# Earlier first steps for the partial sums of a graph layer: 2, 5, 8, 11 tiles in place of 3, 6, 9, 12

## The chip, the cores and the metric

The kernel runs on one core of a Trainium2 chip. The metric is the device time of one execution in microseconds (us). Before the change it is 1529.51 us, the median of three runs (1527.91 to 1533.11).

## What is computed

There are 6250 nodes with 64 features and 206,250 edges, sorted by the node `dst` that they belong to (padded to 206,336 edges, 1612 tiles of 128). For every edge a first layer takes the features of its `dst` node and its own 64 attributes; the hidden rows are then added up by the node `src`, which is in no order; a second layer, a residual and a layer norm follow per node.

```python
msg = jnp.concatenate([src_node_features[col], edge_attr], axis=1)   # col = dst
h = jax.nn.relu(msg @ W1a.T + b1a)
h = h @ W1b.T + b1b
sums = jax.ops.segment_sum(h, row, num_segments=n_nodes)             # row = src
agg = sums / jnp.maximum(counts, 1.0)[:, None]
z = jax.nn.relu(jnp.concatenate([src_node_features, agg], axis=1) @ W2a.T + b2a)
out = jnp.concatenate([z @ W2b.T + b2b, src_node_features], axis=1) @ Wr.T + br
x = _layernorm(x + out)
```

The kernel uses that `W1b` is linear and applies it after the sum, so that what is scattered and summed are rows of 128 hidden values, a 1 for the count and the node's number within its bin (130 floats). Nodes lie in 49 bins of 128.

## The kernel before, in words

**Blocks.** The edges are worked through in 124 blocks of 13 tiles. In a block TensorE (PE) computes the first layer (`hidden`, L1461, one matmul a tile, which the trace shows as two records). ScalarE (ACT) applies the relu into one of `ROWS` = 4 buffers `orow`, used in turn, and puts the node's number beside it (`low_bits`, L1452). VectorE (DVE) and PE work out a slot in DRAM for each row (`bins_of`, `counts_of`, `slots`). GpSimd (POOL) writes each tile of 128 rows into its slots with one indirect DMA (`scatter`, L1513). In blocks 2 to 109, six or nine of the 13 tiles are first joined into groups of four rows of one bin ("fours", `join`, L1348 and L1363, scattered by L1485); the others are "direct rows". So a block has 13 scatters (blocks 0, 1 and 110 to 123), 9 (six tiles joined) or 7 (nine tiles joined: blocks 9, 11, ... 25 and 34, 42, 50, ... 98). The scatters of block k - `LEAD` (2) are written into the program in block k. A row buffer is free for block k once the scatter of block k - 4 has landed.

**Partial sums.** Each bin's rows fill its slots in order, so early tiles of a bin are full long before the last block. `Step` objects say which tiles can be summed from which block on: for each number in `FULL[0]`, a step of direct rows ends at that many tiles of a bin and is ready at the first block by which every bin has at least as many (`low_of`); `FULLQ` does the same for fours. A stage of the two opens `LATE` (3) blocks after the later of them. `groups_of` cuts a stage into groups of at most 3 bins and 12 tiles (`SUMS`, `TILES`). A group is read back from DRAM by SyncE (SP, `read`, L1593, into 9 buffers `rt`), its nodes' numbers are turned into a matrix of ones by DVE (`nodes_of`, L1627), PE multiplies and adds (`summed`, L1647, two records a tile), and `collect` adds the result to `part`.

**What sets the order.** PE, ACT, DVE and SP keep the order in which the program is written. A small planner spreads the groups over the blocks: per block it hands out no more tiles than `RATES` allows (18 in a block with six joined tiles, 10 with nine, 55 with none), and no more than are left divided by the blocks to the next opening:

```python
until = min(o for o in opens if o > k)
credit += min(RATES[joined(k)], max(tiles_in(queue) - credit, 0) / (until - k))
while queue and credit > 0:
    groups_at[k].append(queue.pop(0))
    credit -= tiles_in(groups_at[k][-1:])
credit = min(credit, 0)
```

What the planner gives to block k is read at the end of block k and summed in block k + 1. After block 123 come the groups that are left (`NGR`, 124), then the 17 last groups, three tiles a piece, each followed by the second layer of its bins (`Nodes`).

**src.** The numbers in `src` are loaded into the memory of the `rt` buffers at first; `bins` (L761, L762) splits them into a bin and a place in the bin, in five parts at the blocks of `bins_at`. All of it must be done before `rt` is used for the first read.

Of the kernel before, what the change touches and what calls it, by code (L numbers as in the profile page):

```python
# [453 lines left out]
NEAR = 8  # L454
HEAD = 117
NEXT = 468
FULL = ((3, 6, 9, 12), (1,), ())
BIG = 2.0**20
LATE = 3
RD = 6  # L460
# [14 lines left out]
PACED = range(PRE, 123)  # L475
SIDES, ENATS, CHUNK = 2, 2, 2
ON_ACT = 1
FULLQ = (3, 6, 9, 11, 13)
NODES = 8
FIRST = 4  # L480

# [8 lines left out]
def fast_path(  # L490
# [39 lines left out]
    NT = srcT.shape[1]  # L530
# [35 lines left out]
    def by_bin(of_bin, of_rest):  # L566
        return [of_bin] * (NB - 1) + [of_rest]
# [9 lines left out]
    def low_of(b, n, first=0):  # L577
        _, mean, dev = edges_of(b, n, first)
        return max(0, int(mean - dev)) // P
# [9 lines left out]
    def quads_low(b, n):  # L589
        _, mean, dev = quads_of(b, n)  # L590
        return max(0, int(mean - dev)) * QUAD // P
# [10 lines left out]
    for e, n in enumerate(EPOCHS):  # L602
# [15 lines left out]
        ep_.steps, lo = [], by_bin(0, 0)  # L618
        for t in FULL[e]:
            at = next(k for k in range(n) if low_of(0, k, ep_.first) >= t)  # L620
# [24 lines left out]
    qep.steps, lo = [], by_bin(0, 0)  # L645
    for t in FULLQ:
        at = next(k for k in range(qep.end + 1) if quads_low(0, k) >= t)
# [129 lines left out]
    with (  # L777
# [253 lines left out]

        NBAD = 15 + 5 * NE + 2 * sum(map(len, FULL)) + 2 * len(FULLQ)
        bad = const.tile([P, NBAD], F32, name="bad")
# [797 lines left out]
        nodes_at = {AHEAD_FROM + EVERY * i: b0 for i, b0 in enumerate(range(0, NB, CHUNK))}  # L1831
        assert JOIN_FROM - 3 < AHEAD_FROM - 1 and max(nodes_at) < JOIN_TO

        bins_at = {NEAR - 2: (HEAD, NEXT), 22: (NEXT, 754), 24: (754, 1040), 26: (1040, 1326), 28: (1326, NT)}
        range_at = {4: (0, ALU.min), 5: (1, ALU.max)}
        assert NEXT % (SEG * BLK) == 0 and NEXT // BLK > max(bins_at) + 3
        for g in range(3):
# [392 lines left out]
```

## Time and profile before

| what | us |
|---|---|
| median of three runs | 1529.51 |
| lowest, highest | 1527.91, 1533.11 |
| the profiled execution, its time | 1534.22 |
| its span from the first to the last instruction | 1532.4 |
| PE busy | 1440.7 (94%) |
| DVE busy | 1341.7 (88%) |
| POOL busy | 1128.8 (74%) |
| ACT busy | 1114.6 (73%) |

The profile is that of one execution. Busy shares are means over the span. Time in which an engine issues a DMA does not count as busy, which matters for POOL here. A row of the timeline joins neighbours of one kind: start, duration, engine, line, operation, and how many records; in brackets stands how long the engine was idle before, and what ended that.

### The profile page before, as it was taken

The page shows a single profiled execution, that of the slowest core. Times are in us where ns is not written, and L with a number is a line of the kernel's source. Part 1 is how long each engine was busy: PE and PEld are TensorE (multiplying, and loading weights), DVE is VectorE, ACT ScalarE, POOL GpSimd, SP SyncE. Part 2 cuts the span into 40 slices and gives each one's busy share as a digit, 9 for nine tenths or more (in the row PEclk, how much of TensorE's full clock was granted, in tenths as well). Part 3 has the DMA queues.
Part 4 walks back from the last instruction along what each step waited for, and adds up shares of the span by engine and source line. Part 5 has one row for each costly group of instructions (what it writes and reads, how often), then busy time and mean ns, then how long its engine had stood idle before and what let it go on. Part 6 is the DMA issues. An engine that isn't in the chain of part 4 may idle for free.

```text
span 1532.4 us, 33764 instructions
## 1 busy us (share of the span) xinstructions
PE 1440.7 (94%) x11008; PEld 1274.8 (83%) x11008; DVE 1341.7 (88%) x2882; ACT 1114.6 (73%) x2413; POOL 1128.8 (74%) x1198
## 2 busy tenths in 40 slices
PE   5989999987999999999989998999999999999997
PEld 4767777766888988888878888989888899999896
DVE  8789999887898988979889898999999988788787
ACT  3689999996898888878878887887887744332004
POOL 6777777777777777777777777777777777777734
PEclk9899999998999999999999999999999999999999
DMA  8798998967788888777877767777677899999884
GB/s 206 221 301 284 302 303 288 308 188 257 238 262 256 251 253 270 221 229 224 231 238 214 233 213 244 237 227 250 210 242 229 279 322 320 345 343 310 264 275 115
DMA packets 255427, 390.92 MB, mean 255 GB/s; under 512 B 43412, under 2 KB 186838, under 8 KB 255242
## 3 DMA queue, kind: packets, MB, share of 16 engines
q1 hardware_dynamic: 206874, 265.50, 58.7%
q0 software_dynamic: 47840, 122.94, 22.8%
q8 instruction: 90, 1.47, 0.4%
q14 instruction: 95, 0.78, 0.2%
q10 hardware_dynamic: 528, 0.22, 0.1%
HBM read 213.72 MB, written 174.78 MB: 254 GB/s over the span
## 4 chain that ended last, share of the span: by engine, by line
PE 57%; DMA 16%; ACT 11%; DVE 7%; issue 5%; POOL 2%; SPq 1%; DVEq 0%; ACTq 0%; POOLq 0%
PE place L1647 22%; PE place L1348 11%; DMA rows<-orow,rowidx 9%; PE place L1461 9%; PE place L1363 8%; DMA rt<-rows 3%; DMA rows<-orow,qidx 3%; ACT orow L1366 2%; ACT marks L1314 2%; ACT marks L1318 1%; DVE marks L1302 1%; POOL rows L1513 1%; DVE oh L1627 1%; ACT orow L1465 1%; ACT rhs L1414 1%
## 5 line engine op out<-in xcount | busy, mean ns | idle before, releaser
L1513 POOL DMA_INDIRECT rows<-orow,rowidx x910 | 878.3, 965 | 288.0 <-issue 142.5
L1647 PE MATMUL place<-rt,oh 128*128 128x129 f32 x3952 | 483.7, 277 | 15.3 <-ACT orow L1366 5.9
L1647 PEld LDWEIGHTS place<-rt,oh 128*128 128x128 f32 x3952 | 467.7, 193 | 27.2 <-DVE oh L1627 8.3
L1627 DVE TENSOR_TENSOR oh<-ramp,rt 128x768 f32<-128x768 bf16 (+4 forms) x391 | 309.6, 824 | 42.4 <-DMA rt<-rows 41.3
L1465 ACT ACTIVATE orow<-place 128x512 f32<-128x512 f32 (+2 forms) x263 | 142.5, 542 | 224.5 <-PE place L1461 219.3
L1485 POOL DMA_INDIRECT rows<-orow,qidx x234 | 226.1, 966 | 71.3 <-issue 19.8
L1302 DVE TENSOR_TENSOR marks<-quad_ramp,ramp 128x1024 fp32r<-128x1024 f32 x234 | 273.4, 1213 | 1.5 <-ACT z_act L1310 1.5
L1363 PE MATMUL place<-mv,rj 128*128 128x130 f32 x1872 | 242.7, 280 | 33.9 <-ACT orow L1465 20.6
L1348 PE MATMUL place<-marks,side 128*128 128x512 f32 x702 | 267.5, 410 | 0.0
L1461 PE MATMUL place<-mv,rhs 124*128 124x128 f32 x1820 | 262.5, 289 | 4.7 <-ACT orow L1465 3.8
L1363 PEld LDWEIGHTS place<-mv,rj 128*128 128x128 f32 x1872 | 223.1, 192 | 44.5 <-ACT orow L1465 24.5
L1348 PE MATMUL place<-marks,rest 128*64 128x512 f32 x702 | 240.2, 396 | 0.0
L1461 PEld LDWEIGHTS place<-mv,rhs 124*128 124x128 f32 x1820 | 229.6, 197 | 6.2 <-ACT orow L1465 4.0
L1348 PEld LDWEIGHTS place<-marks,side 128*128 128x128 f32 x702 | 134.3, 191 | 51.6 <-issue 2.0
L1366 ACT ACTIVATE orow<-place 128x260 f32<-128x260 f32 x468 | 163.7, 389 | 13.4 <-PE place L1363 4.1
L1314 ACT ACTIVATE marks<-quad_ramp,z_act 128x512 fp32r<-128x512 f32 x234 | 168.9, 722 | 6.1 <-PE place L1348 2.7
L1318 ACT ACTIVATE marks<-marks,ones 128x512 fp32r<-128x512 f32 x234 | 169.8, 725 | 4.1
L1121 DVE TENSOR_TENSOR_SCAN had<-ramp,bins 128x400 bf16<-128x400 bf16 (+2 forms) x124 | 127.2, 1026 | 13.7 <-ACT orow L1452 1.7
L1353 ACT COPY rj<-place 128x512 f32<-128x512 f32 x234 | 133.3, 570 | 1.9 <-PE place L1348 1.9
L1348 PEld LDWEIGHTS place<-marks,rest 128*64 128x64 f32 x702 | 96.0, 137 | 38.6 <-issue 0.8
L1414 ACT ACTIVATE rhs<-rhs,ones 60x896 f32<-60x896 f32 (+2 forms) x116 | 123.7, 1066 | 3.7
L1412 ACT ACTIVATE rhs<-rhs,from_win 60x896 f32<-60x896 bf16 (+2 forms) x116 | 123.6, 1065 | 2.9
(197 smaller groups left out, 1594.7 us busy)
## 6 DMA issues: line engine op xcount, KB each, us to landing
rt<-rows SPq DMA_DIRECT2D x194, 390.0 KB
rt<-rows SPq DMA_DIRECT2D x97, 325.0 KB
rows<-padrow SPq DMA_DIRECT2D x24, 1040.0 KB
rhs<-in_edgeT SPq DMA_DIRECT2D x90, 224.0 KB
enat<-in_edgeJ SPq DMA_DIRECT2D x90, 192.0 KB
rows<-orow,rowidx POOLq DMA_INDIRECT x910
rt<-rows SPq DMA_DIRECT2D x40, 260.0 KB
rt<-rows SPq DMA_DIRECT2D x48, 195.0 KB
```

The lines of the kernel that those rows point to most:

```text
L1302: nc.vector.tensor_tensor(m[:, :n, :], all_q[:, None, :].to_broadcast([P, n, QUAD * P]), z[:, :n, None].to_broadcast([P, n, QUAD * P]), op ...
L1314: nc.scalar.activation(m[:, t, :], all_q, AF.Square, bias=z_acts[k][:, i * JOIN + t : i * JOIN + t + 1], scale=-1.0)
L1318: nc.scalar.activation(m[:, t, :], m[:, t, :], AF.Relu, bias=ones[:, :1], scale=-1.0)
L1348: done[k, f"turn{i}"] = nc.tensor.matmul(ps[: w.shape[1], :], w, m[:, t, :], start=t + p == 0, stop=last and p == 1).ins.name
L1363: done[k, f"join{i}"] = nc.tensor.matmul(ps[:, j, :], rj[:, (g0 + j) * P : (g0 + j + 1) * P], m, start=True, stop=True).ins.name
L1366: nc.scalar.activation(mrow[:, g0 : g0 + 2, :], ps, AF.Relu)
L1461: done[k, c] = nc.tensor.matmul(ps[:, j, :], rhs[:WIDE, of * P : (of + 1) * P], m[:WIDE, :H], start=True, stop=True).ins.name
L1465: nc.scalar.activation(orow_of(k, k0, n)[:, :, :H], ps[:, :n, :], AF.Relu)
L1485: s = nc.gpsimd.indirect_dma_start(out=qep.rows.rearrange("(q r) f -> q (r f)", r=QUAD), out_offset=bass.IndirectOffsetOnAxis(ap=qidx[:, q ...
L1513: s = nc.gpsimd.indirect_dma_start(out=ep_.rows, out_offset=bass.IndirectOffsetOnAxis(ap=rowidx[:, k % RING * BLK + j : k % RING * BLK + j ...
L1627: nc.vector.tensor_tensor(res[:, at_tile : at_tile + nb * n, :], ramp[:, None, :].to_broadcast([P, nb * n, P]), node[:, :, None].to_broadc ...
L1647: m = nc.tensor.matmul(of_bin(b), oh[:, at, :], rows, start=i == 0, stop=i == len(of) - 1)
```

## The change

The change gives new values to two tables of ends, and moves the last four parts of `src` four blocks ahead, to 18, 20, 22 and 24 from 22, 24, 26 and 28.

```diff
-FULL = ((3, 6, 9, 12), (1,), ())
+FULL = ((2, 5, 8, 11), (1,), ())
...
-FULLQ = (3, 6, 9, 11, 13)
+FULLQ = (2, 5, 8, 11, 13)
...
-        bins_at = {NEAR - 2: (HEAD, NEXT), 22: (NEXT, 754), 24: (754, 1040), 26: (1040, 1326), 28: (1326, NT)}
+        bins_at = {NEAR - 2: (HEAD, NEXT), 18: (NEXT, 754), 20: (754, 1040), 22: (1040, 1326), 24: (1326, NT)}
```

By the rules above, the four stages of direct rows and fours now open at blocks 24, 50, 75 and 99 (33, 58, 83 and 107 before), and hold 194, 294, 292 and 294 tiles (292, 293, 293 and 244 before). The stage behind them, which ends a bin's rows of the first 110 blocks, still opens at 113 and holds 534 tiles and not 486. All stages together hold 1976 tiles as before.

In SP's queue this is block 24 of the change against before (reads are L1593, the other rows are the loads of the blocks 26 and 27).

```order
 L1402 DMA mv<-ytab 60x128
 L870 DMA enat_164<-in_edgeJ 128x384
+L1593 DMA rt<-rows_64 128x3x260 x2
 L863 DMA rhs_145<-in_edgeT 64x896
 L1395 DMA rhs_145<-relt 60x2x448
```

Two reads come between the loads, where before the first read came nine blocks later.

On PE the number of tiles summed ahead of a block's last first-layer matmul shifts as follows, counted in the two orders of its instructions:

| block | 33 | 48 | 83 | 99 | 109 | 123 | in all |
|---|---|---|---|---|---|---|---|
| before | 0 | 174 | 585 | 855 | 1001 | 1680 | 1976 |
| now | 68 | 180 | 578 | 780 | 954 | 1656 | 1976 |

This is PE's order at block 123 before, from the third group of first-layer matmuls (L1461) on; each L1647 row is a group of sums with its number of tiles.

```order
L1461 MATMUL place_151<-mv,rhs_148 128x128 x3
L1647 MATMUL place_149<-rt,oh 128x129 x10
L1461 MATMUL place_153<-mv,rhs_148 128x128 x3
L1647 MATMUL place_150<-rt,oh 128x129 x10
L1647 MATMUL place_151<-rt,oh 128x129 x10
L1647 MATMUL place_153<-rt,oh 128x129 x6
L1647 MATMUL place_152<-rt,oh 128x129 x9
L1647 MATMUL place_149<-rt,oh 128x129 x3
```

And this is the same place now.

```order
L1461 MATMUL place_152<-mv,rhs_148 128x128 x3
L1461 MATMUL place_153<-mv,rhs_148 128x128 x3
L1647 MATMUL place_149<-rt,oh 128x129 x11
L1461 MATMUL place_151<-mv,rhs_148 128x128 x3
L1647 MATMUL place_152<-rt,oh 128x129 x11
L1647 MATMUL place_153<-rt,oh 128x129 x11
L1647 MATMUL place_151<-rt,oh 128x129 x11
L1647 MATMUL place_150<-rt,oh 128x129 x11
L1647 MATMUL place_149<-rt,oh 128x129 x6
L1647 MATMUL place_152<-rt,oh 128x129 x9
```

Behind the last first-layer matmul four groups of 11 stand before the groups of 6 and 9, where there were two groups of 10.

## Rows read from the trace of the kernel before

**Rows 1.** The page's first lines: the span, and busy time of each engine

```profile
span 1532.4 us, 33764 instructions
PE 1440.7 (94%) x11008; PEld 1274.8 (83%) x11008; DVE 1341.7 (88%) x2882; ACT 1114.6 (73%) x2413; POOL 1128.8 (74%) x1198
```

**Rows 2.** The costliest groups, POOL's scatters: count, busy us, mean ns, idle before

```profile
L1513 POOL DMA_INDIRECT rows<-orow,rowidx x910 | 878.3, 965 | 288.0 <-issue 142.5
...
L1485 POOL DMA_INDIRECT rows<-orow,qidx x234 | 226.1, 966 | 71.3 <-issue 19.8
```

**Rows 3.** Timeline of POOL, first, late and last scatters; what follows

```profile
11.08 1.18 POOL L1513 DMA_INDIRECT rows<-orow,rowidx  x1 [6.50 <-DVE rowidx L1269]
...
91.48 0.96 POOL L1513 DMA_INDIRECT rows<-orow,rowidx  x1 [2.54 <-ACT orow L1366]
...
262.53 0.96 POOL L1513 DMA_INDIRECT rows<-orow,rowidx  x1 [1.05 <-DMA rows<-orow,rowidx]
...
1467.27 0.96 POOL L1513 DMA_INDIRECT rows<-orow,rowidx  x1 [0.30 <-issue]
1484.16 0.82 POOL L2056 TENSOR_TENSOR agg<-part,rc 128x384 f32<-128x384 f32 x1 [15.93 <-issue]
```

**Rows 4.** Timeline of PE, from block 123's last first-layer matmuls to the last groups

```profile
1420.60 0.83 PE L1461 MATMUL place<-mv,rhs 124*128 124x128 f32 x6
1421.27 18.98 PE L1647 MATMUL place<-rt,oh 128*128 128x129 f32 x147
...
1479.83 3.18 PE L1647 MATMUL place<-rt,oh 128*128 128x129 f32 x27
1483.18 0.94 PE L1647 MATMUL place<-rt,oh 128*128 128x129 f32 x6 [0.18 <-DVE oh L1627]
```

**Rows 5.** Busy us by stretch: PE, PEld, DVE, ACT, POOL; clock, DMA share, GB/s

```profile
320.00:400.00 80.00, 67.84 (x461) 56.83 (x460) 60.81 (x130) 62.86 (x138) 60.79 (x64) 0.94 0.67 213
...
925.00:1214.00 289.00, 283.03 (x2231) 254.23 (x2231) 269.54 (x549) 233.28 (x484) 219.48 (x229) 0.99 0.76 237
1214.00:1421.00 207.00, 205.06 (x1802) 201.60 (x1801) 167.63 (x324) 79.23 (x113) 156.98 (x165) 1.00 1.00 325
1421.00:1483.00 62.00, 59.84 (x500) 56.85 (x499) 51.97 (x99) 1.98 (x3) 35.92 (x38) 1.00 0.94 290
```

**Rows 6.** By stretch, the sums (L1647) alone: PE and PEld busy, records

```profile
925.00:1214.00 289.00, 103.01 (x830) 99.53 (x829) 0.99 0.76 237
...
1214.00:1483.00 269.00, 216.62 (x1854) 211.00 (x1854) 1.00 0.99 317
```

**Rows 7.** Timeline of PE, last first-layer matmuls of blocks 81, 83, 99, 109

```profile
890.46 0.91 PE L1461 MATMUL place<-mv,rhs 124*128 124x128 f32 x6
...
913.29 0.91 PE L1461 MATMUL place<-mv,rhs 124*128 124x128 f32 x6
...
1101.86 0.91 PE L1461 MATMUL place<-mv,rhs 124*128 124x128 f32 x6
...
1213.29 0.83 PE L1461 MATMUL place<-mv,rhs 124*128 124x128 f32 x6
```

**Rows 8.** Timeline of POOL, last scatters of blocks 81, 83, 99, 109

```profile
925.68 1.23 POOL L1513 DMA_INDIRECT rows<-orow,rowidx  x1 [0.30 <-issue]
...
946.25 0.95 POOL L1513 DMA_INDIRECT rows<-orow,rowidx  x1 [0.30 <-PE cnt_ps L1167]
...
1123.45 0.96 POOL L1513 DMA_INDIRECT rows<-orow,rowidx  x1 [0.30 <-PE place L1348]
...
1237.40 0.95 POOL L1513 DMA_INDIRECT rows<-orow,rowidx  x1 [0.30 <-PE place L1647]
```

**Rows 9.** Timeline of ACT, the first write into block 84's row buffer

```profile
923.20 0.20 ACT L1452 CAST orow<-lo 128x7 f32<-128x7 bf16 x1 [3.80 <-DMA rows<-orow,qidx]
```

**Rows 10.** Busy us by stretch, the slice with the most bytes moved

```profile
1320.00:1360.00 40.00, 39.66 (x350) 38.97 (x350) 30.91 (x50) 12.67 (x18) 30.24 (x33) 1.00 1.04 347
```

## The prediction

> **What bounds the kernel now.** I read the page's busy times first. PE is at 94% and POOL at 74% [rows 1], which points to PE. The costliest groups correct that: POOL has 910 + 234 = 1144 scatters of 0.965 us, and next to each stands idle time of about 0.3 us (288.0 us over 910) that mostly nothing releases [rows 2], so it belongs to the scatter. The timeline of POOL shows the consequence: first scatter at 11.08, last at 1467.27, that is 1456.2 us for 1143 steps, 1.274 us each, and after 91.48 only one wait, of 1.05 us, that is longer than the usual 0.3 [rows 3]. POOL paces blocks 0 to 123, and nothing that the other engines save there brings its last scatter, done at 1468.2, forward.
>
> The end is set by another engine. PE finishes the first layer of block 123 at 1421.4 and then does nothing but sums until 1483.0; the first of the last 17 groups starts at 1483.18 after 0.18 us of waiting [rows 4], and POOL's first work on its nodes is at 1484.16, 15.93 us after the last scatter [rows 3]. So a backlog of sums on PE, and not the last scatter, ends the main part; the 49.2 us behind it (1532.4 - 1483.2) are a pipeline that the change does not touch. The table by stretches says how long PE has been full: it is idle for 6.0 us of 289 from 925 to 1214, 1.9 of 207 to 1421, 2.2 of 62 to 1483 [rows 5]. What PE is given after about 925 us is therefore paid at the end.
>
> How far PE is ahead of POOL is read from two timelines, for each block the end of its last first-layer matmul against the end of its last scatter (blocks are counted off by 26, 14 or 8 records on PE and 13, 9 or 7 scatters on POOL) [rows 7, 8]: 926.9 - 891.4 = 35.5 us at block 81, 947.2 - 914.2 = 33.0 at 83, 1124.4 - 1102.8 = 21.6 at 99, 1238.4 - 1214.1 = 24.3 at 109. This lead has a ceiling, since a row buffer is free only when the scatter four blocks back has landed: ACT waits 3.80 us for such a landing in block 84 [rows 9].
>
> **The change part by part.** The number of tiles to be summed stays at 1976, and all scatters stay. Of the groups, 8 go (17 of three bins in the first stage for 25 of two), and with them 8 additions and 16 reads; these are work of DVE and SP, which PE's sums cover: all of PE's waiting, for DVE too, is 4.1 us from 1214 on [rows 5]. I count them as nothing; without that cover, they would be a few us at most, since the tiles that DVE compares stay the same. What the change really does is to hand the tiles to other blocks, and I go through three stretches.
>
> *Blocks 24 to 48.* 68 tiles now stand ahead of block 33's end. A tile costs PE 216.62 / 1854 records x 2 = 0.234 us [rows 6], so that is 15.9 us, and from 320 to 400 PE has 12.2 us of idle time [rows 5] to put it in. But the first stage must now last until block 50, and at block 48 both orders have done nearly the same (174 and 180 tiles). Nothing is left of it, and since POOL does not wait there, it shows nowhere. The same holds for the parts of `src`: moved four blocks, same work, done before the first read as before. If the 1.05 us wait at 262.5 comes from it, that much could go or double; it is POOL's, and POOL has 15 us of slack against PE at the end.
>
> *Blocks 83 to 99.* Here before does 855 - 585 = 270 tiles and the new order 780 - 578 = 202, since the planner now has until block 99 for the third stage and hands out about 12 a block instead of 18. The 75 tiles that stand behind at block 99 are 17.5 us of PE work. PE could keep them as lead, 21.6 + 17.5 = 39.1 us, but the ceiling was seen at 33 to 35.5. I take 33.0 at block 99; 6 us of PE's time go idle.
>
> *Blocks 99 to 109.* Before does 146 tiles and gains 2.7 us of lead; now it is 174, and 28 x 0.234 = 6.6 us more, so 33.0 + 2.7 - 6.6 = 29.1 us. A wait at the ceiling like that of block 84, where the same rise of the rate stood before, would make it 25.3. I take the middle, 27.2: PE is through with block 109 at about 1211, 3 us earlier than before.
>
> *From there to the end.* 1925 tiles are due before the last groups. Before, 924 of them are left at block 109, now 971: 47 x 0.234 = 11.0 us more, on an engine that has 4.1 us of idle time in these 269 us [rows 5], which I leave as it is. Sum: + 11.0 - 3.0 = + 8.0 us; sums end at 1491 and not 1483. POOL still has no reason to wait: in blocks 112 to 122 its 13 scatters take 13 x 1.274 = 16.6 us, PE's 55 tiles 12.9 us plus what else a block holds (269.0 - 216.6 us that are not sums [rows 6], over 14 blocks, 3.7), and block 123's first layer is late by about half of the 11 us out of a lead of 46.8.
>
> The bounds of this sum: with the ceiling's 35.5 us all the way to block 109, PE is 11.2 us early and the 11.0 are gone; if all 4.1 us of idle time were filled too, the end would come at - 4.3. With no lead gained at all and tiles at the 0.248 us of 925 to 1214 (103.01 / 830 x 2 [rows 6]) on the 47, it is + 11.7; one more stall of 3.8 us for reads that come late makes + 15.5.
>
> One rule of the Trainium skill speaks about this stretch. The trace has 325 GB/s at a DMA share of 1.00 from 1214 to 1421 [rows 5], and 347 GB/s at the highest slice [rows 10]. "DMA: Bandwidth & Descriptors" (Where 436 GB/s comes from) gives about 358 GB/s as what a core gets of its HBM; by that figure, an estimate, 47 tiles of 66,560 bytes would take 8.7 us whatever PE does, and the trace's 347 is in line with such a limit.
>
> **The rivals.** (a) *The transfers bind.* From 1214 on the DMA share is 1.00, and reads come for 53 tiles a block; if the queues and not PE set the pace, PE's lead is worth nothing, and 47 tiles x 66,560 bytes = 3.1 MB more at the 325 GB/s of that stretch are + 9.6 us. For it: the share; against: PE waits 1.9 us in 207. It gives about 1539. (b) *The lead is kept.* If PE holds 33 us or more at block 109, the 47 tiles are all but bought by the time that was won, and the end moves by + 11.0 - 8.7 = + 2.3 or less: 1532 or less, no change that can be told. For it: the stretch to 109 has no blocks of nine joined tiles, which press the lead; against: Rows 7 and 8 show 21.6 and 24.3 where the rate is 15 to 17 tiles a block, and it becomes 17.4. (c) *Faster.* The one way to gain is for PE to reach block 109 with more than 24.3 + 11.0 = 35.3 us of lead, about the most that was seen, and then to fill its idle time as well: - 4.3 us, 1525. For it: groups of 11 and 12 tiles where 10 stood have fewer seams. Against: the row buffers. (d) *The early sums hold up POOL.* POOL waited for ACT at 91 us [rows 3], and sums add work from block 24 on. But each us that POOL loses there eats only its slack of 15 us, so this would take stalls of more than 15 us in all; + 0 otherwise. This is the way in which the change would do nothing.
>
> **How the numbers follow.** The profiled execution took 1534.22 us, 4.7 above the median of 1529.51 us; I add the difference of + 8.0 to the median: 1537.5. A change of less than 0.3% (4.6 us) either way is about what a measurement of this kernel cannot tell from none. Chances: the forecast, + 5 to + 11.7, 0.52; (a) 0.12; a heavier end, up to + 15.5, 0.04; (b), with (d), 0.25; (c), or something that I do not see, 0.07. So slower 0.68, same 0.25, faster 0.07. The range leaves out (c) and the worst stall: from - 1 to + 15, 1528.5 to 1544.5; the forecast's own is 1534.5 to 1541.
>
> **What would show it.** The scatters should still run from 11 to about 1468 us without waits; PE should have little or no idle time left between 320 and 400, and several us of new idle time between blocks 83 and 99, where ACT's casts wait for landings. The lead should be about 33 us at block 99 and 25 to 29 at 109. After block 123's first layer, 24 tiles more are left, and the first of the last groups starts at about 1491, not 1483, at an unchanged distance from the end. If instead the lead at 109 is 33 or more, the middle step is wrong; if PE waits for reads (`oh` for `rt`) after 1214, it is rival (a); if POOL has waits of several us in blocks 24 to 60, (d). An end of the sums before 1483 would refute the whole argument.

## The result: 1547.97 us, 1.1% slower, and the profile after

The changed kernel takes 1547.97 us, the median of six runs (1545.46 to 1549.13). The kernel before takes 1529.79 us in six runs beside them (1527.91 to 1533.11). The ratio is 1.0110, with a 95% interval of 1.0096 to 1.0124. The forecast was 1537.5 us: slower, as it says, but by more than twice the 8 us.

The two profiled executions took 1534.22 and 1549.04 us. They are 14.8 us apart where the medians are 18.2 apart, since the one before is 4.4 us above its median and the one after 1.1. What follows splits the difference of the two traces; some 3 us of the medians' difference lie outside it.

In two of the rounds reported below the kernel before took 1907.51 and 1925.08 us, with 604.1 us of idle time before POOL's scatters in a trace there in place of 288.0 (no_pace_before), on chips numbered 1 and 12 like those of two rounds with 1531.94 and 1532.77 us, so each run is compared with the kernel before of its own round.

The first lines of the page after, which answer to [rows 1], and the larger of its two groups of scatters (busy us, mean ns | idle before, releaser):

```profile
span 1547.3 us, 33676 instructions
PE 1447.7 (94%) x11008; PEld 1280.4 (83%) x11008; DVE 1337.3 (86%) x2866; ACT 1112.6 (72%) x2405; POOL 1130.1 (73%) x1198
...
L1513 POOL DMA_INDIRECT rows<-orow,rowidx x910 | 880.1, 967 | 294.2 <-issue 141.4
```

The scatters cost what they did [rows 2], but POOL's idle time before them is 6.2 us more (294.2 - 288.0). The timeline of POOL shows one new long wait, which accounts for it.

```profile
321.42 0.96 POOL L1485 DMA_INDIRECT rows<-orow,qidx  x1 [0.30 <-issue]
329.74 0.96 POOL L1513 DMA_INDIRECT rows<-orow,rowidx  x1 [7.36 <-PE place L1461]
...
1245.74 0.96 POOL L1513 DMA_INDIRECT rows<-orow,rowidx  x1 [0.30 <-DMA rows<-orow,rowidx]
...
1475.66 0.96 POOL L1513 DMA_INDIRECT rows<-orow,rowidx  x1 [0.30 <-issue]
1498.65 0.83 POOL L2056 TENSOR_TENSOR agg<-part,rc 128x384 f32<-128x384 f32 x1 [22.04 <-issue]
```

One step from 321.42 to 329.74 takes 8.32 us, where a step takes about 1.27: a loss of 7.05 us. Block 109's last scatter ends at 1246.7, 8.3 us later than in [rows 8], and the last scatter of all at 1476.6, 8.4 us later than in [rows 3]; the 1.3 us or so beside the one step are spread over many. The timeline of PE at the same places:

```profile
321.86 1.20 PE L1647 MATMUL place<-rt,oh 128*128 128x129 f32 x4 [7.70 <-DVE oh L1627]
324.05 2.95 PE L1647 MATMUL place<-rt,oh 128*128 128x129 f32 x12 [0.99 <-DVE oh L1627]
...
328.58 0.89 PE L1461 MATMUL place<-mv,rhs 124*128 124x128 f32 x6
...
1218.67 0.83 PE L1461 MATMUL place<-mv,rhs 124*128 124x128 f32 x6
...
1431.71 0.83 PE L1461 MATMUL place<-mv,rhs 124*128 124x128 f32 x6
1432.38 27.24 PE L1647 MATMUL place<-rt,oh 128*128 128x129 f32 x214
1460.01 37.49 PE L1647 MATMUL place<-rt,oh 128*128 128x129 f32 x330 [0.39 <-DVE oh L1627]
1497.68 0.94 PE L1647 MATMUL place<-rt,oh 128*128 128x129 f32 x6 [0.18 <-DVE oh L1627]
```

The first of the last groups starts at 1497.68, 14.5 us later than in [rows 4]. The 14.5 us split at block 109. POOL is 8.3 us late there. PE's lead over POOL is 1246.7 - 1219.5 = 27.2 us, where it was 24.2, which takes 3.0 off. From block 109 to the first last group it is 278.2 us where it was 269.1, so + 9.1 us. 8.3 - 3.0 + 9.1 = 14.4. What lies behind has hardly moved (1547.3 - 1497.7 = 49.6 us, 49.2 before).

Busy us by stretch (PE, PEld, DVE, ACT, POOL; clock, DMA share, GB/s), which answers to [rows 5]:

```profile
320.00:400.00 80.00, 75.00 (x553) 65.18 (x554) 69.15 (x153) 63.79 (x139) 55.33 (x57) 0.95 0.74 224
1214.00:1421.00 207.00, 204.85 (x1795) 200.99 (x1795) 170.41 (x313) 81.20 (x115) 157.16 (x164) 1.00 1.01 329
1219.50:1498.00 278.50, 275.68 (x2395) 269.20 (x2393) 227.71 (x420) 81.16 (x116) 195.23 (x204) 1.00 1.00 320
```

In the last stretch PE is idle for 2.8 us of 278.5. The sums alone answer to [rows 6]:

```profile
1219.50:1498.00 278.50, 227.51 (x1950) 221.84 (x1951) 1.00 1.00 320
```

They are 10.9 us more than the 216.62 before, for 96 records, that is 48 tiles.

Where POOL's long wait comes from is read backwards. DVE waited for the reads of the group (timeline of DVE):

```profile
320.80 0.96 DVE L1627 TENSOR_TENSOR oh<-ramp,rt 128x768 f32<-128x768 bf16 x1 [8.55 <-DMA rt<-rows]
```

And SP's timeline has these reads (L1593) behind seven transfers that clear slots of `rows` (L1573):

```profile
304.08 7.77 SPq L1573 DMA_DIRECT2D rows<-padrow  x7
311.89 2.77 SPq L1593 DMA_DIRECT2D rt<-rows  x2
```

The chain of waits runs through just that, from the second of these reads (start, us, what):

```profile
313.26 9.75 DMA rt<-rows
323.04 0.97 DVE oh L1627
```

So the reads that block 27 issues, for sums that the new order puts into block 28, leave SP behind the clearing, land near 321 and 323, and PE, which keeps its order, stands for 7.70 us with the rest of block 28's first layer behind it. The table by stretches shows what else happens there (columns as above):

```profile
312.00:322.00 10.00, 2.30 (x17) 2.01 (x18) 1.21 (x2) 6.01 (x14) 7.56 (x9) 0.76 1.05 305
322.00:330.00 8.00, 7.01 (x39) 6.21 (x40) 5.43 (x12) 0.50 (x2) 0.64 (x2) 0.66 0.72 227
```

While PE stands, the DMA engines are full (share 1.05). Behind the stand the granted clock is 0.66 on the mean of 8 us, so part of them at the lower of its two levels (1.2 GHz), and 12 records of sums take 2.95 us. At the 0.117 us a record of [rows 6] they would take 1.4, so on these records alone PE's wait costs it an estimated 1.5 us more than its 7.70. What POOL then waits for, and where its loss goes, was open.

### The profile page after: what moved, and what is told of

Same layout as the page of the kernel before. It is cut to its first block, busy times and chain, and to the rows that moved or that the text cites. A ratio compares the mean times of both kernels' runs of the same rounds, so it can differ in the third digit from the quotient of the medians.

```text
span 1547.3 us, 33676 instructions
## 1 busy us (share of the span) xinstructions
PE 1447.7 (94%) x11008; PEld 1280.4 (83%) x11008; DVE 1337.3 (86%) x2866; ACT 1112.6 (72%) x2405; POOL 1130.1 (73%) x1198
## 4 chain that ended last, share of the span: by engine, by line
PE 61%; DMA 14%; ACT 10%; DVE 7%; issue 5%; POOL 1%; SPq 1%; ACTq 0%; DVEq 0%; POOLq 0%
PE place L1647 22%; PE place L1348 13%; PE place L1461 9%; PE place L1363 8%; DMA rows<-orow,rowidx 6%; DMA rt<-rows 4%; DMA rows<-orow,qidx 3%; ACT marks L1314 2%; DVE marks L1302 2%; ACT orow L1366 1%; ACT orow L1465 1%; DVE oh L1627 1%; ACT marks L1318 1%; ACT rhs L1414 1%; ACT rhs L1412 1%
## 5 line engine op out<-in xcount | busy, mean ns | idle before, releaser
L1513 POOL DMA_INDIRECT rows<-orow,rowidx x910 | 880.1, 967 | 294.2 <-issue 141.4
L1647 PE MATMUL place<-rt,oh 128*128 128x129 f32 x3952 | 489.7, 279 | 22.5 <-DVE oh L1627 13.7
L1647 PEld LDWEIGHTS place<-rt,oh 128*128 128x128 f32 x3952 | 472.8, 194 | 35.6 <-DVE oh L1627 10.7
L1465 ACT ACTIVATE orow<-place 128x512 f32<-128x512 f32 (+2 forms) x263 | 142.5, 542 | 221.4 <-PE place L1461 217.3
L1461 PE MATMUL place<-mv,rhs 124*128 124x128 f32 x1820 | 261.2, 288 | 0.8 <-DVE rhs L1420 0.8
L1461 PEld LDWEIGHTS place<-mv,rhs 124*128 124x128 f32 x1820 | 228.4, 196 | 2.2 <-DVE rhs L1420 1.1
```

Source lines behind the costliest of these rows:

```text
L1461: done[k, c] = nc.tensor.matmul(ps[:, j, :], rhs[:WIDE, of * P : (of + 1) * P], m[:WIDE, :H], start=True, stop=True).ins.name
L1465: nc.scalar.activation(orow_of(k, k0, n)[:, :, :H], ps[:, :n, :], AF.Relu)
L1513: s = nc.gpsimd.indirect_dma_start(out=ep_.rows, out_offset=bass.IndirectOffsetOnAxis(ap=rowidx[:, k % RING * BLK + j : k % RING * BLK + j ...
L1647: m = nc.tensor.matmul(of_bin(b), oh[:, at, :], rows, start=i == 0, stop=i == len(of) - 1)
```

## The experiments

Theory A was: POOL's wait and the backlog of later sums are two separate losses, and POOL's is found whole at the end. Its rivals: POOL's loss is eaten by its slack of 15 us, as the prediction had it, and all of the 15 us are sums; or the sums in early blocks cost as such, without any wait.

**late_first: the change, with its first stage opened at block 33 as before.**

```diff
+        open_at[0] = 33
         opens = sorted(...)
```

> The changed kernel, with its first stage opened at block 33 as before, so that no read stands in SP's queue beside the clearing transfers of blocks 25 and 27; all later stages as changed. Theory A: the result is made of two terms, a wait of POOL near 325 us (8.3 us) that goes through to the end, and sums that are handed to later blocks (+9.1 us from block 109 on, less 3.0 us of lead). Then this kernel loses the first term only: last scatter at about 1467 to 1468 us of the span, first of the last groups at 1489 to 1491, time about 1536 to 1539 us, ratio to before 1.004 to 1.006. Theory B: POOL's wait is eaten by its 15 us of slack at the end, and the later sums and reads alone make the result. Then it stays at 1546 to 1549, ratio 1.011.

It takes 1536.75 us (1534.12 to 1540.22), a ratio of 1.0037 (1.0021 to 1.0053). POOL keeps its step of about 1.26 near 325. Its last scatter, and below it PE's first last group:

```profile
1468.02 0.96 POOL L1513 DMA_INDIRECT rows<-orow,rowidx  x1 [0.31 <-issue]
```

```profile
1489.64 0.94 PE L1647 MATMUL place<-rt,oh 128*128 128x129 f32 x6 [0.18 <-DVE oh L1627]
```

The last scatter is where it was before, and the sums end 6.5 us later. So the later sums alone cost 5.7 us by the ratio, and the other 11.2 us of the change (1547.97 - 1536.75) hang on the first stage. POOL's one step is 7.05 of these by the trace; where the rest lies is not shown.

**clears_early: the change, with the clearing in blocks 5 to 19 and not up to 27.**

```diff
-        clears = {5 + 2 * i: (0, i) for i in range(CLEAR)}
+        clears = {k: (0, i) for i, k in enumerate((5, 6, 7, 9, 10, 11, 13, 14, 15, 17, 18, 19))}
```

> The changed kernel, with the twelve clearing transfers of the first rows issued by block 19 and not by block 27 (blocks 5, 6, 7, 9, 10, 11, 13, 14, 15, 17, 18, 19); the first reads stay at block 24. Theory A with the clears as the cause of POOL's wait: the reads of blocks 24 to 28 land within a few us, POOL has no wait over 2 us near 325 us, time 1536 to 1540 us, ratio 1.004 to 1.007. If the wait is due to the reads' own number or to the other loads, it stays at 5 us or more, and the ratio at 1.009 to 1.012. The clears may in turn press the blocks before 20, where the DMA share is 0.9 to 1.0: if POOL waits there, the time does not fall.

It takes 1557.92 us (1550.34 to 1559.0), a ratio of 1.0160 (1.0127 to 1.0192): slower than the change. The wait near 325 is gone, as expected; but POOL now has eight waits of 1.1 to 6.0 us in blocks 9 to 25. The longest stands here, with the last scatter:

```profile
264.73 0.96 POOL L1513 DMA_INDIRECT rows<-orow,rowidx  x1 [6.03 <-ACT z_act L1310]
...
1484.89 0.96 POOL L1513 DMA_INDIRECT rows<-orow,rowidx  x1 [0.30 <-issue]
```

The longest follows the seven transfers that stood in block 27, now in block 19 (SP's timeline):

```profile
240.35 7.61 SPq L1573 DMA_DIRECT2D rows<-padrow  x7
```

Behind them ACT waits 6.99 us, to 261.72, for a load (`enat`). In blocks 24 to 30, where no clearing is left, PE has no wait of 0.5 us or more for reads. As a repair it failed. It still speaks for A: the last scatter is 17.6 us later than before, the lead at block 109 is 27.5 us as with the change, and the span is 1557.1. What POOL loses in the first fifth of the run stays lost.

**pause27 and pause115: the kernel before, with idle work for POOL between the scatters of block 27, and of block 115.**

```diff
+        def pause(k):
+            nc.gpsimd.tensor_copy(idle, orow_of(k, 6, 7))
+            for i in range(7):
+                nc.gpsimd.memset(idle, float(i))
...
+            if k - LEAD == 27:      # 115
+                pause(k - LEAD)
```

> The kernel before, with one copy and seven memsets of 128 x 910 floats on POOL between the scatters of block 27, some 7 to 9 us in all, nothing else changed (the results go nowhere). Theory A: PE's lead on POOL has a ceiling of four row buffers, so by block 83 PE is as far ahead as before, counted from POOL, and the whole pause is found again in the last scatter, in block 109's first layer and in the time: + 6 to + 9 us, ratio 1.004 to 1.006. Theory B, the prediction's: POOL's loss eats its slack of 15 us at the end, sums end at 1483 as before, time within 2 us of before, ratio 0.999 to 1.001.

> The kernel before, with the same pause of POOL between the scatters of block 115. Theory A: from block 110 on PE is not held by row buffers (its lead grows from 24 to 47 us) and the end is set by the backlog of sums, so here the pause is eaten by the slack: last scatter 7 to 9 us later, sums end at 1483 to 1485, time within 2 us of before, ratio 0.999 to 1.001. If every us of POOL counts wherever it is lost: + 6 to + 9 us, ratio 1.004 to 1.006, as for the pause at block 27.

Eight scatters take 2.0 us a step in place of 1.26, so POOL loses some 6 us. pause27 takes 1540.97 us, a ratio of 1.0066 (1.0044 to 1.0089): about 10 us by the medians, 5.9 by the spans of the profiled runs. The two agree once the executions are placed: the profiled one of the kernel before is 3.1 us above the median of this round (1531.17), that of pause27 0.9 below its own. In four traces of kernels that have POOL's work up to block 109 as before and no pause there (bins_only_b, no_pace_before_b, spread_b, pause115) block 109's last scatter ends at 1234.5 to 1236.6 us; in pause27 it ends at 1242.4, so the pause of 6 us is there in full. pause115 takes 1537.97 us, 1.0037 (1.0008 to 1.0065). I had expected the late pause to be eaten, as PE's backlog is what ends the main part, and it was not. PE's timeline in pause115 shows why:

```profile
1447.53 16.90 PE L1647 MATMUL place<-rt,oh 128*128 128x129 f32 x134 [7.61 <-DVE oh L1627]
...
1487.11 0.94 PE L1647 MATMUL place<-rt,oh 128*128 128x129 f32 x6 [0.18 <-DVE oh L1627]
```

The chain of waits there shows what PE's wait was for (start, us, what):

```profile
1439.18 2.75 DMA rows<-orow,rowidx
...
1442.19 4.23 DMA rt<-rows
```

And this is PE at the same place in the kernel before:

```profile
1444.86 1.38 PE L1647 MATMUL place<-rt,oh 128*128 128x129 f32 x10 [1.71 <-DVE oh L1627]
```

The last stage before the end is read once block 121 has been scattered (1435.4 us before, 1440.1 with the pause), with 38 us of sums behind it. Before, PE runs dry there by 1.71 us, and SP issues no read from 1435.2 to 1438.4. So POOL had no 15 us to give: at its end both engines were tight.

**first_only_b: the kernel before, with an end at 2 tiles added and `src` early; the later stages stay as they were.**

```diff
-FULL = ((3, 6, 9, 12), (1,), ())
+FULL = ((2, 3, 6, 9, 12), (1,), ())
-FULLQ = (3, 6, 9, 11, 13)
+FULLQ = (2, 3, 6, 9, 11, 13)
```

> The change's early part alone (stages of two tiles at block 24 and one tile at block 33, src worked up by block 24; from block 58 on the sums of before), again, beside a kernel before of about 1530 us. Theory A: POOL waits near 325 us as in the changed kernel, and what it loses there is found in the end: + 6 to + 11 us, ratio 1.004 to 1.007. Theory B (a wait of POOL is eaten, only later sums cost): ratio 0.999 to 1.001.

It takes 1554.36 us (1551.84 to 1555.63), a ratio of 1.0138 (1.0121 to 1.0156). The direction is as A has it, the size is not: I had overlooked that a stage that must be done in nine blocks is handed out at the full rate, which makes three waits of POOL out of one.

```profile
306.04 0.96 POOL L1513 DMA_INDIRECT rows<-orow,rowidx  x1 [5.16 <-PE place L1461]
...
337.06 0.96 POOL L1513 DMA_INDIRECT rows<-orow,rowidx  x1 [8.36 <-PE place L1461]
...
345.66 0.96 POOL L1513 DMA_INDIRECT rows<-orow,rowidx  x1 [4.88 <-PE place L1647]
...
1488.46 0.96 POOL L1513 DMA_INDIRECT rows<-orow,rowidx  x1 [0.30 <-issue]
```

The last scatter is 21.2 us late, the lead at block 109 is that of before (24.3 us), and the span is 20.5 us longer. Here POOL's loss is the whole of it, and passes on one for one.

**bins_only_b: the kernel before, with `src` early and nothing else.**

```diff
-        bins_at = {NEAR - 2: (HEAD, NEXT), 22: (NEXT, 754), 24: (754, 1040), 26: (1040, 1326), 28: (1326, NT)}
+        bins_at = {NEAR - 2: (HEAD, NEXT), 18: (NEXT, 754), 20: (754, 1040), 22: (1040, 1326), 24: (1326, NT)}
```

> The kernel before with src worked up by block 24 and nothing else changed, again, beside a kernel before of about 1530 us. Both theories: no difference, ratio 0.998 to 1.002, POOL's one wait of 1 us moves from 260 to about 245 us. If this part presses blocks 19 to 28, POOL has waits of several us there and the ratio is 1.003 or more.

1531.79 us, a ratio of 0.9992 (0.9981 to 1.0004): nothing, as the prediction had it. It does lower PE's lead at block 24 from 25.1 to 22.6 us; the change has 22.1.

**reads_first_b: the change, with a block's reads put ahead of its clearing on SP.**

```diff
+            issue(k)
             if k in clears:
                 clear(*clears[k])
-            issue(k)
```

> The changed kernel, with the reads of a block put into SP's queue ahead of that block's clearing transfers (it matters in blocks 25 and 27). It ran once on a chip where the kernel before took 1907 us and POOL had 184 steps of over 2 us; that says nothing of a wait of 8 us, so it runs again beside a kernel before of about 1530 us. Theory A: in the changed kernel the reads of block 27 stood behind seven clearing transfers, so PE waited 7.7 us and POOL 7.4; with the reads in front POOL has no wait over 2 us near 325 us, its last scatter ends at 1468 to 1470, ratio 1.003 to 1.006. If clears hold up reads by filling the DMA engines, whatever the order in the queue, POOL waits 4 us or more there and the ratio is 1.009 or above.

It takes 1540.88 us (1533.88 to 1543.52), a ratio of 1.0048 (1.0032 to 1.0063). POOL has no wait over 2 us near 325, and its last scatter ends at 1470.7. The reads leave 11.6 us earlier on SP's timeline:

```profile
300.33 1.14 SPq L1593 DMA_DIRECT2D rt<-rows  x2
301.51 10.62 SPq L1573 DMA_DIRECT2D rows<-padrow  x7
...
318.38 2.19 SPq L1593 DMA_DIRECT2D rt<-rows  x2
```

Yet PE still waits, a block later and for the reads of 318.38:

```profile
326.71 1.20 PE L1647 MATMUL place<-rt,oh 128*128 128x129 f32 x4 [5.46 <-DVE oh L1627]
```

So with the other order the stand comes a block later and is shorter (5.46 us for 7.70). The seven clearing transfers, two of 1040 KB, four of 260 and one of 65, are 3.26 MB, an estimated 10.7 us at the 305 GB/s of that stretch, and reads on either side of them share the engines with them. That this load makes the stand is likely, since it goes with the clearing in clears_early; how much of it is the load and how much the order is not shown. Whether POOL feels it is a matter of PE's lead, and this run is just at the edge. These are the last first-layer matmuls (PE) and the last scatter (POOL) of block 29:

```profile
332.84 1.63 PE L1461 MATMUL place<-mv,rhs 124*128 124x128 f32 x6
...
346.25 0.96 POOL L1485 DMA_INDIRECT rows<-orow,qidx  x1 [0.31 <-issue]
```

The lead is 347.2 - 334.5 = 12.7 us, and POOL just does not wait. The sums of the early blocks are all still here, 32 tiles by block 28 as with the change, and the ratio is within the noise of late_first's 1.0037: without POOL's wait, early sums as such cost nothing that shows.

**no_pace_after_b and its control: POOL without the written dependency.** The program also ties a scatter of block k to the first layer of block k + 1 (`PACED`; tile 8 of a block with six joined tiles waits for the last first-layer matmul of the next). The wait at 329.74 is one of these. So a new theory A' ("theory A" in the two texts below) said that this tie, and not late rows, costs the 7.4 us.

```diff
-PACED = range(PRE, 123)
+PACED = (*range(PRE, 22), *range(34, 123))
```

> The changed kernel without the added dependency of the scatters of blocks 22 to 33 on the next block's first layer, once more (the first run stood on a chip on which the kernel before takes 1925 us). Theory A: POOL's wait of 7.36 us at 329.74 was for this written dependency and goes, block 27's scatters end at 324 to 326 (330.7 with the change), the last scatter comes at 1468 to 1470, ratio to the kernel before 1.0035 to 1.005. Theory B: the rows themselves are late, and the ratio stays at 1.009 to 1.012, the last scatter at 1475 or later.

> Control, once more: the kernel before with the same edit. There was no wait of POOL over 2 us in blocks 22 to 33, so no difference, 0.998 to 1.002.

The change without the tie takes 1548.06 us (1541.43 to 1554.08), a ratio of 1.0103 (1.0075 to 1.0132); the control 1530.84, 0.9992 (0.9980 to 1.0004). A' falls as the cause of the loss. POOL's timeline shows that the wait only moved:

```profile
325.98 0.99 POOL L1513 DMA_INDIRECT rows<-orow,rowidx  x1 [0.30 <-issue]
333.62 0.95 POOL L1513 DMA_INDIRECT rows<-orow,rowidx  x1 [6.65 <-ACT z_act L1310]
...
339.99 0.96 POOL L1513 DMA_INDIRECT rows<-orow,rowidx  x1 [2.89 <-ACT orow L1366]
```

POOL goes on for a few scatters, to 326.97, and then stands for rows of block 28, which ACT writes here (ACT's timeline):

```profile
332.86 0.49 ACT L1465 ACTIVATE orow<-place 128x384 f32<-128x384 f32 x1 [14.97 <-PE place L1461]
```

And PE's timeline, with its first layer of block 28 at the end:

```profile
323.52 1.20 PE L1647 MATMUL place<-rt,oh 128*128 128x129 f32 x4 [9.54 <-DVE oh L1627]
...
331.22 1.59 PE L1461 MATMUL place<-mv,rhs 124*128 124x128 f32 x6
```

The rows themselves were late, by a stand that was longer here (9.54 us for 7.70) and by a low clock behind it: the last six records of block 28's first layer take 1.59 us and not 0.89. The granted clock is 0.53 there (columns as in the result):

```profile
324.00:336.00 12.00, 11.10 (x46) 9.20 (x45) 8.43 (x29) 2.58 (x6) 4.27 (x5) 0.53 0.47 152
```

Tied or not, PE's wait is POOL's.

**spread_b: the kernel before with ends at 3, 6, 8, 10 and 12, to bring sums forward at the end instead.**

```diff
-FULL = ((3, 6, 9, 12), (1,), ())
+FULL = ((3, 6, 8, 10, 12), (1,), ())
-FULLQ = (3, 6, 9, 11, 13)
+FULLQ = (3, 6, 8, 10, 12, 13)
```

> The kernel before with its stages ending at 3, 6, 8, 10, 12 tiles (fours 3, 6, 8, 10, 12, 13), again, beside a kernel before of about 1530 us: 49 tiles more are summed by the end of block 109. Theory A2 (POOL's pace, through the scatter of block 121 that the last stage's reads wait for, is as tight as the backlog): 0 to - 2 us, ratio 0.998 to 1.001, and PE waits longer than the 1.7 us of before at about 1443 us. If the backlog alone sets the end: up to - 9 us, ratio 0.994 to 0.996.

With `bins_at` as before it takes 1531.02 us, a ratio of 0.9996 (0.9982 to 1.0011). Fewer sums at the end bring nothing that shows. In its trace 56 tiles more are summed by the end of block 109, which is 13.1 us at 0.234 us. PE's lead there is 19.4 us for 24.2, so 4.8 us are paid by then, and from there on PE waits longer (columns as in the result, then PE's timeline):

```profile
1215.20:1478.00 262.80, 253.81 (x2187) 246.37 (x2186) 208.81 (x397) 80.48 (x115) 189.07 (x198) 1.00 0.98 309
```

```profile
1438.07 2.28 PE L1647 MATMUL place<-rt,oh 128*128 128x129 f32 x18 [1.71 <-DVE oh L1627]
```

It is idle for 9.0 us where it was for 4.1 [rows 5]. The wait at the place that A2 names is 1.71 us, as long as before, and with the two behind it (0.94 and 0.78) 3.4 us; five others, of 0.6 to 1.5 us, lie between 1250 and 1370. So A2 had the time right, but that these waits are all for POOL's last scatters is not shown. No version here beats the kernel before.

**The first runs of six of these kernels** stand beside a kernel before of 1907.51 us (the first four) and 1925.08 us (the last two). The runs above are the second ones. What was expected of the first:

> The changed kernel, with the reads of a block put into SP's queue ahead of that block's clearing transfers (it matters in blocks 25 and 27; nothing else is moved). Theory A: the reads of block 27 landed late because they stood behind seven clearing transfers (issued from 304.1 to 311.9 us), so PE waited 7.7 us for them and POOL 7.4; with the reads in front PE waits under 2 us there, POOL has no wait over 2 us near 325 us, its last scatter ends at 1468 to 1470, and the time is that of the kernel with the late first stage, ratio 1.003 to 1.006. If the clears hold up reads merely by filling the 16 DMA engines, whatever the order in the queue, POOL still waits 4 us or more and the ratio stays at 1.009 or above.

> The change's early part alone: a first stage of two tiles that opens at block 24 and src worked up by block 24, then a stage of one tile at block 33, and from block 58 on the stages of before (ends 2, 3, 6, 9, 12; fours 2, 3, 6, 9, 11, 13). From block 58 on each block does the sums it did before, so nothing is handed to later blocks. Theory A: POOL waits near 325 us as in the changed kernel (5 to 9 us; the first stage is handed out at the full rate here, so perhaps in more places), and the time rises by that: + 6 to + 11 us, ratio 1.004 to 1.007. Theory B (a wait of POOL is eaten, only the later sums cost): within 2 us of before, ratio 0.999 to 1.001.

> The kernel before, with src worked up by block 24 (blocks 18, 20, 22, 24) and nothing else changed. Both theories: the same work four blocks earlier, with PE 22 us ahead of POOL there; a wait of POOL of 1 us near 260 us may move to 245 us; no difference, ratio 0.999 to 1.001. If this part is what presses the blocks 19 to 28, POOL has waits of several us there and the ratio is 1.003 or more.

> The kernel before with its stages of direct rows ending at 3, 6, 8, 10, 12 tiles and fours at 3, 6, 8, 10, 12, 13: blocks 75 to 107 get about 12 tiles each where before had 12 up to block 83 and 18 from there; 49 tiles more are summed by the end of block 109. Theory A2: in the kernel before POOL's pace and the backlog of sums are both tight at the end, since the last stage's reads wait for the scatter of block 121 (done at 1435.4 us) and PE stood idle for 1.7 us at 1443 us waiting for them; less backlog then only makes PE wait longer there, and the time falls by 0 to 2 us, ratio 0.998 to 1.001. If the backlog alone sets the end, 49 tiles of 0.234 us less give up to - 9 us, ratio 0.994 to 0.996.

> The changed kernel, with the scatters of blocks 22 to 33 free of the added dependency on the first layer of the block behind (PACED), all else as it is. Theory A: PE still waits about 7 us for the reads of block 27, but its lead over POOL's data, about 13 us at block 28, covers that; POOL's wait of 7.36 us at 329.74 was for this written dependency (tile 8 of block 27 for the last first-layer matmul of block 28) and goes. Then POOL's block 27 ends at 324 to 326 (330.7 with the change, 323.2 before), the last scatter at 1468 to 1470, and the time is that of the two runs in which the wait was absent, a ratio of 1.0035 to 1.005 to the kernel before. Theory B: the rows themselves are late, POOL waits for ACT's write of block 28 instead, at most some scatters later; the ratio stays at 1.009 to 1.012 and the last scatter at 1475 or later.

> The kernel before with the same edit of PACED, as a control: no wait of POOL over 2 us near blocks 22 to 33 was there to go, so theory A expects no difference, ratio 0.998 to 1.002. If it gains 3 us or more by itself, the other run has to be read against this one and not against the kernel before.

The ratios were 0.9964 (0.9937 to 0.9992), 1.0048 (1.0019 to 1.0076), 0.9978 (0.9955 to 1.0001), 1.0097 (1.0061 to 1.0133), 1.0045 (1.0024 to 1.0065) and 1.0019 (0.9998 to 1.0040), in this order. Where they differ from the second runs, I go by the second.

## Why the prediction was wrong

The step that failed is the one on blocks 24 to 48: "Nothing is left of it, and since POOL does not wait there, it shows nowhere." It rested on two things, and both were wrong.

First, that POOL would not wait. I had set 15.9 us of sums against 12.2 us of PE's idle time and compared totals at block 48, but not followed the lead from block to block, as I did from 81 on. These are the last first-layer matmuls and the last scatter of block 24 with the change, and block 28's last scatter:

```profile
268.94 0.89 PE L1461 MATMUL place<-mv,rhs 124*128 124x128 f32 x6
...
290.98 0.95 POOL L1513 DMA_INDIRECT rows<-orow,rowidx  x1 [0.30 <-issue]
...
341.34 0.96 POOL L1513 DMA_INDIRECT rows<-orow,rowidx  x1 [0.30 <-issue]
```

A lead of 22.1 us, as block 24 has it, is no cover of 22.1 us, since it contains the scatters that POOL still has to make for that block (nine of them are 11.4 us; neighbouring blocks interleave, so the count is good to a few scatters). The runs show where it ends: POOL stands at a lead of 12.8 us at block 28 with the change (342.3 - 329.5), and does not at 12.7 in reads_first_b, so some 9 to 10 us were in hand. By block 28 the sums (32 tiles, 7.5 us at 0.234 us), four waits ahead of sums (1.25 + 1.87 + 7.70 + 0.99 = 11.8 us; the profile puts the first down to ACT, the others to reads) and the low clock behind them (an estimated 1.5 us) took more than that: 20.8 us. The leads agree: before, it rose by 4.3 us from block 24 to 28 (25.1 to 29.4), and with the change it fell by 9.3 although POOL itself lost 7.05, which is 20.7 us in all. What made the longest of them was the clearing in block 27's part of SP's queue, and I had looked at block 24 alone.

Second, the dismissal of rival (d): "each us that POOL loses there eats only its slack of 15 us". The 15.93 us between the last scatter and the next work on POOL [rows 3] are no slack. Up to block 109 PE can't run ahead of POOL by more than the row buffers allow, so when POOL is 8.3 us late, PE is late with it: its lead at block 109 was 27.2, 27.5 and 26.8 us in the change, clears_early and pause27, with POOL between 4.0 and 17.6 us later there than in the trace before. And at the end the last stage waits for block 121's scatters, as pause115 showed. Rival (d) was right about the place and the cause, and its price was not nothing: POOL's loss passes on whole. By its test in the prediction, waits of several us in blocks 24 to 60, the first trace shows it.

The rest of the sum held in its size, but in part by luck. The lead at block 99 was 32.6 us (33.0 forecast), at block 109 27.2 (27.2; 27.4 to 28.5 in the four other runs with the same later stages). It did not come there on the forecast's way: PE was at 28.2 us and not 33.0 at block 83, and from there kept all of the 15.9 us of the 68 tiles. The several us of new idle time between blocks 83 and 99 are not there (4.2 us, 5.1 before), though ACT waits eight times for landings, 12.1 us in all, where it waited once. The 27.2 was the middle of two values, and a wait of ACT at the ceiling, of 4.7 us, did come behind block 99. From there to the end it is + 9.1 us and not + 11.0: 47 tiles more as counted, 10.9 us of sums, but PE had 1.3 us less idle time than before, which I had left as it was. late_first has this term alone at 6.5 us by the trace and 1.0037 by the runs, against the forecast's 8.0. So of the change's 1.0110, about a third or a bit more is the term that I had forecast (1.0037 to 1.0048 in the two runs without POOL's wait). The rest, 9 to 11 us, goes with POOL's wait, of which the trace shows 7.05 us as one step.

Rival (a), transfers that bind, is out: the DMA share is 1.00 to 1.01 as before, and PE waits only 2.8 us in 278.5. The 347 GB/s of [rows 10] is no limit either: the same trace has 378 GB/s from 1350 to 1360, and first_only_b 374 from 1310 to 1330. Rivals (b) and (c) needed a lead of 33 us and more at block 109.

One reading of [rows 2] was too strong: "mostly nothing releases" the idle time before the scatters, but the profile gives 142.5 of 288.0 us to nothing, about half. The step of 1.27 us, on which the argument rests, does not depend on it.

What stays open: what pause27 costs beyond the 6 us of its pause (1.0044, the low end of its interval, is 6.7 us); where the few us of the first stage's loss lie that POOL's one step does not hold; and how much of the stand in block 28 is the place of the reads in SP's queue and how much the bytes of the clearing. clears_early takes both away from there at once, and reads_first_b changes the place alone.

## What to carry to other kernels

A lead of one engine over another is slack only above what the consumer still has of the block in hand: take the consumer's time for one block off, and follow what is left block by block through every stretch that the change touches, queue of loads included. An engine that paces the work has no slack at its end just because another engine finishes last; ask what the last one reads, and from which of the first one's results on. When work moves to an earlier place, look at what stands ahead of its reads in that place's queue and at the bytes under way there, not only at the place where it begins.

## What was not expected of the hardware

On POOL a memset of 128x910 f32 (0.87 us) beside a scatter raised the step from 1.26 to 2.0 us and not to 2.13: the idle time before the scatter fell from 0.30 to 0.16 us, so part of what a scatter costs beside its 0.96 us runs under other work.

The seven clearing transfers took SP 7.77 us to issue with the change, 1.1 us each, and 10.62 us in reads_first_b, where reads of rows were under way beside them.

A stand of PE cost more than its length: behind 7.70 us of waiting the granted clock was 0.66 on the mean of the next 8 us, and behind 9.54 us in no_pace_after_b 0.53 on the mean of 12 us.
